# A two-layer transformer kernel: the second layer's attention and FFN worked through in pairs of batches instead of single batches

## The chip, the cores and the metric

The kernel runs on one core of a Trainium2 chip. Times are device microseconds (us) of that core for one execution of the whole program. The kernel before takes 736.29 us (median of three runs, 736.03 to 736.33). All data are f32.

A core has several engines that each work through a queue of their own in order: TensorE (PE; the profile lists its weight loads as PEld), VectorE (DVE), ScalarE (ACT), GpSimd (POOL), and SyncE (SP), on whose queue this kernel issues its DMAs. An instruction that waits holds up everything behind it in its own queue. TensorE writes its results into PSUM; a *bank* is the unit of PSUM that the program's tiles are made of.

## What is computed

Four batches of 256 tokens with 256 channels go through two layers, each with attention and an FFN, each behind a layer norm and added to `x`:

```python
x = x + _L0_attn_ref(_layernorm(x), ...)   # 16 heads of 128, window of 128
x = x + _L0_ffn_ref(_layernorm(x), ...)    # silu(gate) * up, two of four kept, down
x = x + _L1_attn_ref(_layernorm(x), ...)   # 16 heads of 128, causal
x = x + _L1_ffn_ref(_layernorm(x), ...)    # silu(W1 x) * (W3 x), Hadamard transform, W2
```

The change touches the second layer. Its attention is

```python
k = jnp.einsum('ihd,bpd->biph', W_K, x)
q = jnp.einsum('ihd,bpd->biph', W_Q, x)
v = jnp.einsum('ihd,bpd->biph', W_V, x)
scores = jnp.einsum('biph,biqh->biqp', k, q)
...
attn = jax.nn.softmax(masked / jnp.sqrt(jnp.float32(d_head)), axis=-1)
z = jnp.einsum('biqp,biph->biqh', attn, v)
...
out = jnp.einsum('df,bqf->bqd', W_O, z_flat)
```

and its FFN is

```python
up_gate = jnp.einsum('bsd,hd->bsh', x, W1)
up_lin = jnp.einsum('bsd,hd->bsh', x, W3)
hidden = fwht(jax.nn.silu(up_gate) * up_lin)
out = jnp.einsum('bsh,dh->bsd', hidden, W2)
```

## The kernel before

**Seven products.** Layer 2's projections are done by a scheme that multiplies two 2×2 block matrices with seven block products instead of eight (`seven_products`, L662–689). Its products are numbered 1 to 7; `left_of` (L636) makes the sums of blocks of the normed, transposed `x` on DVE, `right_of` (L647) those of the weights. Each product goes into one of three PSUM tiles `x`, `y`, `z`, some on top of what is there; ACT copies (`u`, L671–677) and DVE adds (L680–686) take the four result blocks out between the products.

**Attention.** There are 16 units: one batch and a group of four heads, the batch changing fastest. `project1` (L870) makes a unit's q and k by seven products of four matmuls with 128 columns each (L881; the columns are half of a batch's tokens), and its v by seven of one matmul with 256 columns (L887). `probabilities` (L203) multiplies q and k (`sc`, L217/L218), takes the row maxima on DVE (`mx`, L220; `nb`, L225), exponentiates on ACT (L230), takes reciprocals of the sums on DVE (`rs`, L235) and scales on POOL (`p`, L238). `planes` (L247) splits the words on POOL (`pl`, L244) and issues a DMA transpose on SP's queue (`plT`). `joined` (L257) puts the words together again on ACT and DVE (`pT`, L264), and `values` (L270) multiplies with v (`av`, L272/L275). ACT copies the result to `zT`.

`pipelined` (L300) runs the units in steps: step s does project(s), score(s−1) and attend(s−2), and then whatever the dictionary `behind` has for that step. In steps 1 to 17 TensorE's order is as the program writes it; the order on the other engines, and everything in the second FFN, is set by a scheduler. The sums of weight groups 2 and 3 (`load_group1`) are put into a list and taken from it a few at a time between the products of later projections (`pull`). Group 2 is loaded in step 4, group 3 in step 8; each has two buffers in turn.

**Output projection.** For units 0 to 8 it goes by seven products of two matmuls with 128 columns (`out_by_seven`, L787–808), interleaved with project(4) to project(12); POOL makes their left sums (`left_of_z`), DVE adds each product's result to `x` (L807). Units 9 to 15 are projected plainly, eight matmuls of 256 columns in one PSUM bank, out of order: 12 behind step 15, 9 and 10 ahead of attend(14), 11 and 13 ahead of attend(15), and 14 and 15 at the end:

```python
for t in range(NT):
    for j in range(4):
        nc.tensor.matmul(po[:, t, :], lhsT=zT[:, j, t * P : (t + 1) * P], rhs=w[:, j, :], ...)
for t in range(NT):
    nc.vector.tensor_tensor(xt, po[:, t, :], xt, ALU.add)
```

**The way into the second FFN.** `normed` (L150–200) takes a batch's moments on DVE (`st`, `mv`), computes `ve` and `rstd` on POOL (L156/L157), normalises on DVE (`xn`, L171), and transposes: either on TensorE, or by splitting words on POOL (`xpl`), a DMA transpose (`xplT`) and joining on ACT (`xnT`, L197). Batch 0's norm is issued in step 16 by DMA, batch 1's in the first FFN unit on TensorE.

**Second FFN.** Eight units, one batch and half of the 1024 hidden channels. `gated1` (L948) makes gate and up together, in seven products of four matmuls with 128 columns (L959), then silu on ACT and the product on DVE. `down` (L598) projects back, its two token halves in two PSUM banks, interleaved with the next unit's gate and up. W2 carries the Hadamard transform (`hadamard`), prepared during the attention.

Of the kernel before, what the change touches and what calls it, by code (L numbers as in the profile page):

```python
# [14 lines left out]

# [12 lines left out]
P = 128  # L28
# [3 lines left out]
HD = 128  # L32
# [16 lines left out]
def two_layers(ctx, tc, consts, tables, x, wq, wkv, wo, w_gate, w_up, w_down,  # L49
# [230 lines left out]
    def project_out1(po, zT, w, b):  # L280

        for t in range(NT):
            for j in range(4):
                nc.tensor.matmul(  # L284
                    po[:, t, :], lhsT=zT[:, j, t * P : (t + 1) * P], rhs=w[:, j, :],
                    start=(t == j == 0), stop=(j == 3), skip_group_check=True,
                )
        for t in range(NT):
            xt = xs[b * NT + t]
            nc.vector.tensor_tensor(xt, po[:, t, :], xt, ALU.add)  # L290

# [243 lines left out]
    def ffn0():  # L535
        hs, xn = {}, dict(enumerate(xn_f))
        for n in range(8):
            b, gc = divmod(n, 2)
            hs[n] = h = gated(xn[b], gate_sb, up_sb, 4 * gc, "h")
            a = page("a")  # L540
            nc.scalar.activation(a, h, AF.Abs)
            keep_two_of_four(a, h)
            if gc == 0 and b + 2 < B:
                xn[b + 2] = normed(b + 2, by_dma=True)
            if n >= 2:
                run(down(hs, n - 2, down_sb))
            if n == 4:
                xn1[0] = normed(0, by_dma=True)
            if n == 6:
                xn1[1] = normed(1, by_dma=True)  # L550
                left1[0] = left_of(xn1[0])
        return [down(hs, n, down_sb) for n in (6, 7)]
# [45 lines left out]
    def down(hs, n, w, last=False):  # L598


        b, gc = divmod(n, 2)
        if gc == 0:
            pos[b] = [bank([D], "po_f") for _ in range(NT)]
        for t in range(NT):
# [8 lines left out]
            if gc == 1:  # L613
                x = xs[b * NT + t]
                nc.vector.tensor_tensor(x, pos[b][t], x, ALU.add)
                if last:
                    at = (b * NT + t) * P
                    nc.sync.dma_start(out[at : at + P, :], x)
            yield

# [13 lines left out]
    def left_of(xnT):  # L634

        s = late.tile([P, 4, P], F32, tag="xs4", name="xs4", bufs=4)  # L636
        x11, x12, x21, x22 = (xnT[:, c, t * P : (t + 1) * P] for t in range(2) for c in range(2))
        for i, a, b, op in (
            (0, x21, x22, ALU.add), (1, s[:, 0], x11, ALU.subtract),
            (2, x11, x21, ALU.subtract), (3, x12, s[:, 1], ALU.subtract),  # L640
        ):
            nc.vector.tensor_tensor(s[:, i], a, b, op)
        return x11, x12, s[:, 3], x22, s[:, 0], s[:, 1], s[:, 2]
# [9 lines left out]
    def right_of(w11, w12, w21, w22, t, later=False):  # L653

        for i, a, b, op in (
            (0, w12, w11, ALU.subtract), (1, w22, t[0], ALU.subtract),
            (2, w22, w12, ALU.subtract), (3, w21, t[1], ALU.subtract),
        ):
            if later:
                queue.append((t[i], a, b, op))  # L660
            else:
                nc.vector.tensor_tensor(t[i], a, b, op)  # L662
        return w11, w21, w22, t[3], t[0], t[1], t[2]

    def seven_products(product, x, z, y, c11, c12, c21, c22, shape, z_alone=True):


        tag = "u" if len(shape) == 3 else "uv"
        u = [late.tile(shape, F32, tag=tag, name="u", bufs=3) for _ in range(3)]
# [30 lines left out]
    def load_group1(g, later=False):  # L700
# [7 lines left out]
        qk_t = late.tile([P, 4, 2, 2, HD], F32, tag="qkt", name="t_qk")  # L708
        v_t = late.tile([P, 4, 2 * HD], F32, tag="vt", name="t_v")
        gw[g] = (  # L710
            right_of(*(qk[:, :, c, :, m, :] for c in range(2) for m in range(2)),
                     [qk_t[:, i] for i in range(4)], later),
            right_of(*(v[:, c, m, :] for c in range(2) for m in range(2)),
                     [v_t[:, i] for i in range(4)], later),
        )

    def attention1(finish_ffn0):
        left = left1

        def project(n, _):  # L720
            g, b = divmod(n, 4)
            held = project1(
                left[b], gw[g], out_by_seven(n - 4) if 4 <= n < 13 else None,
                {3: turn3} if n == 2 else {},
            )
            if n < 2:
                with tc.issue_after(last_of["sum"].ins):
                    left[b + 1] = left_of(xn1[b + 1])
# [5 lines left out]
            if b == 0 and 1 <= g < 3:  # L734
                load_group1(g + 1, later=True)
            return held

        def score(n, held):
            qk, v = held
            ps = [  # L740
                probabilities(qk[:, 0], qk[:, 1], heads, mask1) for heads in ((1, 3), (0, 2))
            ]
            return [planes(p, page_of_planes) for p in ps], v

        zTs, kept = {}, {14: (9, 10), 15: (11, 13)}

        def attend(n, held):
            ps, v = held
            for m in kept.get(n, ()):
                out(m, True)(zTs)  # L750
            if n in (1, 3, 5, 7):
                zT = late.tile([P, 4, T], F32, tag="zT1", name="zT1", bufs=1)
# [3 lines left out]
            for kk in range(2):  # L756
                pT = joined(ps[kk], ((nc.scalar.copy, slice(0, 2), None),) if n < 1 else (
# [4 lines left out]
                for j in range(2):  # L762
                    hd = 2 * j + 1 - kk
                    values(v[:, 0, hd, :], v[:, 1, hd, :], pT[:, j], av[:, j, :])
                nc.scalar.copy(zT.rearrange("p (j m) t -> p m j t", m=2)[:, 1 - kk], av)
            if n < 9:
                z_left[n] = left_of_z(zT, z_sums[:, n % 2])
# [4 lines left out]
        def left_of_z(z, s):  # L772
            x11, x12, x21, x22 = (
                z[:, 2 * k : 2 * k + 2, t * P : (t + 1) * P] for t in range(2) for k in range(2)
            )
            for i, a, b, op in (
                (0, x21, x22, ALU.add), (1, s[:, 0], x11, ALU.subtract),
                (2, x11, x21, ALU.subtract), (3, x12, s[:, 1], ALU.subtract),
            ):
                nc.gpsimd.tensor_tensor(s[:, i], a, b, op)  # L780
            return x11, x12, s[:, 3], x22, s[:, 0], s[:, 1], s[:, 2]

        def right_of_out(g):
            w, t = w_out[g], w_sums[:, g % 2]
            w_right[g] = right_of(
                *(w[:, 2 * k : 2 * k + 2, m * P : (m + 1) * P] for k in range(2) for m in range(2)),
                [t[:, i] for i in range(4)], later=True,  # L787
            )

        def out_by_seven(n):  # L790


            g, b = divmod(n, 4)
            left, right = z_left[n], w_right[g]
            sums = bank([3, P], "po1")
            x, y, z = (sums[:, i, :] for i in range(3))
            for o, i, t, m in (
# [3 lines left out]
                for j in range(2):  # L801
                    nc.tensor.matmul(  # L802
                        o, lhsT=left[i - 1][:, j, :], rhs=right[i - 1][:, j, :],
                        start=(i == 1 and j == 0), stop=(j == 1), skip_group_check=True,
# [4 lines left out]

        def load_ffn1(_):  # L810
# [3 lines left out]

        def out(n, kept=False):
            g, b = divmod(n, 4)

            def emit(done):
                if not kept:
                    project_out1(bank([NT, D], "po1"), done[n], w_out[g], b)  # L820
                else:
                    with tc.issue_after(last_of[1].ins):
                        project_out1(st([P, NT, D], "po1"), done[n], w_out[g], b)
            return emit
# [10 lines left out]
        def left3(_):  # L835
            with tc.issue_after(last_of["mx"].ins):
                left[3] = left_of(xn1[3])

        behind = {step: [lambda _, g=g: right_of_out(g)] for g, step in enumerate((0, 3, 8))}
        behind[0].append(lambda _: run(finish_ffn0[0]))  # L840
        behind[1] = [lambda _: run(finish_ffn0[1]), norm3]
        behind[2] = [left3]
        behind[8].insert(0, lambda _: load_out(2))
        behind[12] = [load_ffn1, lambda _: load_out(3)]
# [5 lines left out]
        behind.setdefault(11, []).append(prepare)  # L850
        for i in range(12):
            behind.setdefault(11 + i // 4, []).append(
# [3 lines left out]
        def prepare_ffn1(half):  # L856
# [6 lines left out]
        behind.setdefault(15, []).append(out(12))  # L863
        behind[16] = behind.get(16, []) + [
            lambda _: xn_f.append(normed(0, by_dma=True)),
            prepare_ffn1(1),
        ]
        behind[17] = [out(14), out(15)]
        pipelined((project, score, attend), (0, 1, 2), behind, (0, 1, 2), (1, B * 4 + 2))
# [4 lines left out]
    def project1(x, w, between, others):  # L874
        wqk, wv = w
        qk = late.tile([P, 2, 4, T], F32, tag="qk", name="qk1")
        v = late.tile([P, NT, 4, HD], F32, tag="v", name="v1", bufs=3)

        def product_qk(o, i, first):
            for j in range(4):  # L880
                last_of[1] = nc.tensor.matmul(  # L881
                    o[:, j, :], lhsT=wqk[i - 1][:, j // 2, j % 2, :], rhs=x[i - 1],
# [3 lines left out]
        def product_v(o, i, first):  # L886
            last_of[1] = nc.tensor.matmul(  # L887
                o, lhsT=x[i - 1], rhs=wv[i - 1], start=first, stop=True, skip_group_check=True
            )

        c = qk.rearrange("p k (a m) (t c) -> p (k a) m t c", m=2, t=NT)
        products = [seven_products(
            product_qk, *(st([P, 4, P], f"qk_{n}") for n in "xzy"),
            *(c[:, :, m, t, :] for t in range(2) for m in range(2)), [P, 4, P],
        )]
        c = v.rearrange("p t (m j) h -> p t m (j h)", m=2)
# [3 lines left out]
            *(c[:, t, m, :] for t in range(2) for m in range(2)), [P, 256], z_alone=False,  # L900
# [42 lines left out]
    def factors_ffn1(half):  # L943

        t = late.tile([P, 2, 4, 2, P], F32, tag="qkt", name="t_gu")
        r = []
        for i, w in enumerate((w1_sb, w3_sb)):
            w = w[:, :, 4 * half : 4 * half + 4, :].rearrange("p c (a m) f -> p c a m f", m=2)  # L948
            r.append(right_of(*(w[:, c, :, m, :] for c in range(2) for m in range(2)),
                              [t[:, i, k] for k in range(4)], half == 0))  # L950
        return r

    def gated1(x, r, last, between):

        def product(o, i, first):
            for j in range(4):
                nc.tensor.matmul(  # L959
# [142 lines left out]
```

## Time and profile before

| | |
|---|---|
| median of three runs | 736.29 us |
| the profiled execution, its own time | 736.55 us |
| its span | 734.6 us |
| first layer (to about 355 us) | 355 us, PE busy 347.5 |
| 355 to 400 us, the attention's first steps | 45 us, PE busy 44.08 |
| 400 to 620 us, its later steps | 220 us, PE busy 220.00 |
| 620 to 652.4 us, its end | 32.4 us, PE busy 32.32 |
| 652.4 us to the end, second FFN | 82.2 us, PE busy 79.19 |

The span is what lies between the first and the last instruction that the profiler recorded; the time of the same execution is 1.95 us longer. Busy time of an engine in a stretch says how much room it has there: an engine that is busy all of a stretch sets its length, whatever the others do. The last 3.4 us of the span, in which TensorE is done, are the last addition and the transfer of the output.

In the views of the profile, a line of a timeline gives the start, the length, the engine, the line of the program, the operation, the tiles written and read, shape, and how many records are merged in it. What stands in brackets is the time the engine was idle before it, and what ended that. A matmul's own length includes the time that its last results need to arrive; the next one may start before, so that the pitch from start to start is what a stream of them costs. An f32 matmul shows as two records.

### The profile page before, as it was taken

How to read it: one execution, taken by the hardware profiler on the slowest of the kernel's cores; microseconds unless marked ns; L12 is line 12 of the kernel's file. 1: busy time of each engine (PE TensorE's matmuls, PEld its weight loads, DVE VectorE, ACT ScalarE, POOL GpSimd, SP SyncE). 2: the span in 40 equal slices, each digit the busy share in tenths (PEclk: the TensorE clock that was granted, in tenths of full speed). 3: DMA queues.
4: the chain of work that ended last, by engine and by line, in shares of the span. 5: the costliest groups of instructions: out<-in, count | busy, mean ns of one | idle time of the engine just before them, and what ended most of it. 6: DMA issues, size and time to landing. Idle time of an engine off the chain costs nothing.

```text
span 734.6 us, 11900 instructions
## 1 busy us (share of the span) xinstructions
PE 723.1 (98%) x4020; PEld 595.2 (81%) x4020; DVE 478.2 (65%) x1455; ACT 410.4 (56%) x985; POOL 368.0 (50%) x525
## 2 busy tenths in 40 slices
PE   8999999999999999999999999999999999999998
PEld 5556576656666778888988999999998998899997
DVE  6999877887887537987744565556553655454443
ACT  2487887667767952222257555555555676434332
POOL 1588878897799631011115655445446675520000
PEclk9999999999999999999999999999999999999999
DMA  8732344425445445000203632352233522501100
GB/s 324 298 65 49 60 89 85 93 52 94 83 82 101 73 99 202 16 14 15 67 7 62 150 52 54 45 158 44 44 64 56 155 44 45 97 6 22 27 11 30
DMA packets 138349, 57.53 MB, mean 78 GB/s; under 512 B 131504, under 2 KB 133680, under 8 KB 137520
## 3 DMA queue, kind: packets, MB, share of 16 engines
q1 hardware_dynamic: 138288, 56.77, 34.1%
q8 instruction: 32, 0.52, 0.3%
q14 instruction: 29, 0.24, 0.1%
HBM read 22.94 MB, written 1.05 MB: 33 GB/s over the span
## 4 chain that ended last, share of the span: by engine, by line
PE 82%; DVE 8%; issue 4%; ACT 3%; POOL 1%; DMA 1%; SPq 0%; ACTq 0%; DVEq 0%; POOLq 0%
PE pj L457 10%; PE pgu L561 8%; PE po L296 7%; PE qk_x L881 6%; PE po_f L606 6%; PE sc L218 6%; PE gu_x L959 4%; PE po L802 4%; PE av L272 4%; PE po L284 3%; PE av L405 3%; PE qk_y L881 3%; PE v_x L887 3%; PE sc L217 3%; PE v_zy L887 2%
## 5 line engine op out<-in xcount | busy, mean ns | idle before, releaser
L238 POOL TENSOR_SCALAR p<-p,rs 128x128 f32<-128x128 f32 (+1 forms) x256 | 113.6, 463 | 136.3 <-DVE rs L235 136.3
L264 ACT COPY pT<-plT 128x1536 uint16<-128x1536 uint16 (+1 forms) x62 | 90.0, 1508 | 15.7 <-DMA plT<-pl 15.7
L244 POOL TENSOR_SCALAR pl<-p 128x1536 uint16<-128x1536 uint16 x64 | 94.3, 1474 | 4.5 <-POOL p L238 0.5
L220 DVE CUSTOM_DVE_ANT_0 p<-sc,cst 128x128 f32<-128x128 f32 (+1 forms) x256 | 78.7, 352 | 10.0 <-PE sc L218 7.4
L230 ACT ACTIVATE p<-p,nb,r 128x128 f32<-128x128 f32 (+1 forms) x128 | 68.2, 534 | 20.2 <-DVE nb L227 20.2
L457 PE MATMUL pj<-wq,xnT 128*128 128x512 f32 x128 | 61.0, 595 | 1.7 <-DVE qT L519 1.1
L230 ACT ACTIVATE p<-p,nb 128x128 f32<-128x128 f32 (+1 forms) x128 | 56.3, 441 | 9.6 <-DVE nb L225 9.6
L457 PE MATMUL pj<-wkv,xnT 128*128 128x512 f32 x128 | 60.1, 592 | 0.0
L296 PE MATMUL po<-wo,zT 128*128 128x256 f32 x256 | 57.9, 379 | 0.0
L467 ACT ACTIVATE sq<-pj 128x512 f32<-128x512 f32 (+1 forms) x64 | 30.9, 489 | 42.6 <-DVE qc L462 42.3
L689 ACT COPY qk<-qk_x 128x512 f32<-128x512 f32 x16 | 9.4, 585 | 81.0 <-PE qk_x L881 81.0
L296 PEld LDWEIGHTS po<-wo,zT 128*128 128x128 f32 x256 | 48.3, 190 | 7.0 <-ACT kT L530 0.6
L156 POOL TENSOR_SCALAR ve<-mv 128x2 f32<-128x2 f32 (+1 forms) x17 | 4.3, 254 | 89.0 <-DVE mv L152 88.5
L457 PEld LDWEIGHTS pj<-wkv,xnT 128*128 128x128 f32 x128 | 24.3, 190 | 30.2 <-issue 28.5
L462 DVE TENSOR_TENSOR qs<-pj,sin_s 128x512 f32<-128x512 f32 (+1 forms) x64 | 35.3, 551 | 13.5 <-PE pj L457 12.9
L807 DVE TENSOR_TENSOR x<-po,x 128x128 f32<-128x128 f32 x63 | 18.0, 286 | 39.6 <-PE po L802 39.6
L457 PEld LDWEIGHTS pj<-wq,xnT 128*128 128x128 f32 x128 | 23.5, 190 | 24.7 <-issue 20.1
L244 POOL TENSOR_SCALAR qpl<-qc 128x1024 uint16<-128x1024 uint16 x20 | 28.8, 1452 | 18.9 <-PE av L409 8.2
L272 PE MATMUL av<-pT,v 128*128 128x256 f32 x128 | 38.3, 381 | 0.0
L218 PE MATMUL sc<-kT,qT 128*128 128x256 f32 x128 | 38.3, 381 | 0.0
L218 PE MATMUL sc<-qk 128*128 128x256 f32 x128 | 38.2, 380 | 0.0
L500 POOL TENSOR_TENSOR r<-ve,mhalf 128x12 f32<-128x12 f32 x16 | 36.6, 2290 | 0.8
(171 smaller groups left out, 1847.7 us busy)
## 6 DMA issues: line engine op xcount, KB each, us to landing
w<-in_w_dram SPq DMA_DIRECT2D x3, 1024.0 KB, 4.9
wq<-in_wq_dram SPq DMA_DIRECT2D x4, 512.0 KB, 7.5
wkv<-in_wkv_dram SPq DMA_DIRECT2D x4, 512.0 KB, 8.1
wo<-in_wo_dram SPq DMA_DIRECT2D x4, 512.0 KB, 10.3
w_qk<-in_w_q_dram SPq DMA_DIRECT2D x4, 512.0 KB, 4.6
w_qk<-in_w_k_dram SPq DMA_DIRECT2D x4, 512.0 KB, 5.2
w_v<-in_w_v_dram SPq DMA_DIRECT2D x4, 512.0 KB, 6.0
w_o<-in_w_o_dram SPq DMA_DIRECT2D x4, 512.0 KB, 6.6
```

Of the source, the lines that this page charges most:

```text
L218: nc.tensor.matmul(sc[:, P : 3 * P], lhsT=q[:, P:T], rhs=k, start=True, stop=True)
L220: last_of["mx"] = nc.vector.tensor_tensor_reduce(out=p[:, j, cols], in0=sc[:, cols], in1=mask[:, cols], scale=1.0, scalar=-3.0e38, op0=ALU ...
L230: last_of["exp"] = nc.scalar.activation(p[:, j, cols], p[:, j, cols], AF.Exp, bias=nb[:, j, i : i + 1], scale=SCALE1 if rq is None else rq ...
L238: nc.gpsimd.tensor_scalar(p[:, j, cols], p[:, j, cols], rs[:, j, i : i + 1], 1.0, ALU.mult, ALU.mult)
L244: last_of["planes"] = nc.gpsimd.tensor_scalar(o, i, 1.0, 1.0, ALU.mult, ALU.mult)
L264: copy(words.rearrange("p (n w) -> p w n", w=2), halves[:, :, js].rearrange("p w j n -> p w (j n)"),)
L272: nc.tensor.matmul(av, lhsT=v0, rhs=pT[:, 0:T], start=True, stop=False, skip_group_check=True)
L296: nc.tensor.matmul(po, lhsT=zTs[hd // 4][:, hd % 4, t * P : (t + 1) * P], rhs=w[:, hd, :], start=(hd == 0), stop=(hd == n - 1),)
L457: last_of[0] = nc.tensor.matmul(pj, lhsT=xnT[:, c, t * P : (t + 1) * P], rhs=w[:, g, c, :], start=(c == 0), stop=(c == NC - 1),)
L561: nc.tensor.matmul(o[:, j, :], lhsT=w[:, c, f0 + j, :], rhs=xnT[:, c, :], start=(c == 0), stop=(c == NC - 1),)
L606: nc.tensor.matmul(pos[b][t], lhsT=hs[n][:, j, t * P : (t + 1) * P], rhs=w[:, 4 * gc + j, :], start=(gc == 0 and j == 0), stop=(gc == 1 an ...
L881: last_of[1] = nc.tensor.matmul(o[:, j, :], lhsT=wqk[i - 1][:, j // 2, j % 2, :], rhs=x[i - 1], start=(first and j == 0), stop=True, skip_ ...
```

## The change

**Pairs.** A unit of the second attention is now two heads of a group in two batches, and there are still 16 units. A pair of consecutive units (k) is one group g and one pair of batches p: the order of (g, p) is (0,0), (1,0), (0,1), (1,1), (2,0), (2,1), (3,0), (3,1), so that the first two groups take turns. A q or k product is two matmuls with 256 columns in place of four with 128. The v of a group and a pair of batches is made by the two units together, one token half each, and its products stay one matmul of 256 columns. `left_of` makes its sums once for two batches. In the second FFN a unit is a pair of batches and half of the hidden channels, four in all; gate and up have seven products each, in turn, two matmuls of 256 columns per product.

**Output projection.** Eight projections, numbered 0 to 7 (pair k and batch j of the pair), go by seven in steps 5 to 12. Numbers 8 to 15 are plain: 8 behind step 12, 9 behind 13, 12 and 13 behind 15, 10 and 11 ahead of attend(15), 14 and 15 interleaved with the first FFN unit. Score(15) moves from step 16 into step 15, after attend(13). Block t=0 is added to `x` before block t=1 is multiplied, in the same PSUM bank; the second FFN's `down` does likewise, with one bank for both halves (the first FFN keeps the old one as `down0`).

**Blocks and loads.** Sums that nobody reads the original of any more overwrite it: `w12` in `right_of`, `x21` in `left_of`, so three blocks of sums in place of four. Groups 2 and 3 are loaded behind project(5) and project(7). W2 is loaded behind step 10 instead of ahead of the attention. All of the second FFN's norms transpose by DMA; those of batches 0 and 1 are issued together in step 16.

```diff
-    def project_out1(po, zT, w, b):
+    def project_out1(po, heads, w, b):
         for t in range(NT):
-            for j in range(4):
+            for j, z in enumerate(heads):
                 nc.tensor.matmul(
-                    po[:, t, :], lhsT=zT[:, j, t * P : (t + 1) * P], rhs=w[:, j, :],
+                    po[:, t, :], lhsT=z[:, t * P : (t + 1) * P], rhs=w[:, j, :],
                     start=(t == j == 0), stop=(j == 3), skip_group_check=True,
                 )
-        for t in range(NT):
+                if j == 1:
+                    yield
             xt = xs[b * NT + t]
             nc.vector.tensor_tensor(xt, po[:, t, :], xt, ALU.add)
+            yield
...
     def down(hs, n, w, last=False):
+        p, half = divmod(n, 2)
+        for k in range(2):
+            b = 2 * p + k
+            if half == 0:
+                pos[b] = bank([NT, D], "po_f")
+            for t in range(NT):
+                for j in range(4):
+                    nc.tensor.matmul(
+                        pos[b][:, t, :], lhsT=hs[n][k][:, j, t * P : (t + 1) * P],
+                        rhs=w[:, 4 * half + j, :], start=(half == t == j == 0),
+                        stop=(half == 1 and j == 3), skip_group_check=True,
+                    )
+                    if j == 1:
+                        yield
+                if half == 1:
+                    x = xs[b * NT + t]
+                    nc.vector.tensor_tensor(x, pos[b][:, t, :], x, ALU.add)
+                    if last:
+                        at = (b * NT + t) * P
+                        nc.sync.dma_start(out[at : at + P, :], x)
+                yield
...
-        for i, a, b, op in (
-            (0, w12, w11, ALU.subtract), (1, w22, t[0], ALU.subtract),
-            (2, w22, w12, ALU.subtract), (3, w21, t[1], ALU.subtract),
+        for piece in (
+            (t[0], w22, w12, ALU.subtract), (w12, w12, w11, ALU.subtract),
+            (t[1], w22, w12, ALU.subtract), (t[2], w21, t[1], ALU.subtract),
         ):
...
     def attention1(finish_ffn0):
+        def unit(n):
+            k, a = divmod(n, 2)
+            g, p = (k % 2, k // 2) if k < 4 else divmod(k, 2)
+            return g, p, a
+
         def project(n, _):
-            g, b = divmod(n, 4)
-            held = project1(
-                left[b], gw[g], out_by_seven(n - 4) if 4 <= n < 13 else None,
+            g, p, a = unit(n)
+            qk, vs[g, p, a] = project1(
+                left[p], gw[g], a, out_by_seven(*divmod(n - 5, 2)) if 5 <= n < 13 else None,
                 {3: turn3} if n == 2 else {},
             )
...
-            if b == 0 and 1 <= g < 3:
-                load_group1(g + 1, later=True)
-            return held
+            if n in (5, 7):
+                load_group1((n - 1) // 2, later=True)
+            return qk
...
+        def score_last(_):
+            scored[15] = score(15, qk_of[15])
...
-        zTs, kept = {}, {14: (9, 10), 15: (11, 13)}
+        zTs, kept, qk_of = {}, {15: (10, 11)}, {}
...
+        behind[10].extend((lambda _: load_out(2), load_w2))
+        behind[12].extend((load_ffn1, lambda _: load_out(3), out(8)))
+        behind[13].append(out(9))
...
-        behind.setdefault(15, []).append(out(12))
-        behind[16] = behind.get(16, []) + [
-            lambda _: xn_f.append(normed(0, by_dma=True)),
+        behind[15].extend((score_last, out(12), out(13)))
+        behind[16].extend((
+            lambda _: xn_f.extend(normed(b, by_dma=True) for b in range(2)),
             prepare_ffn1(1),
-        ]
-        behind[17] = [out(14), out(15)]
-        pipelined((project, score, attend), (0, 1, 2), behind, (0, 1, 2), (1, B * 4 + 2))
+        ))
+        pipelined((keep_qk, score, attend), (0, 1, 2), behind, (0, 1, 2), (1, B * 4 + 2))
+        return chain(*(product_out(n, bank([NT, D], "po1")) for n in (14, 15)))
...
         def product_qk(o, i, first):
-            for j in range(4):
+            for j in range(2):
                 last_of[1] = nc.tensor.matmul(
-                    o[:, j, :], lhsT=wqk[i - 1][:, j // 2, j % 2, :], rhs=x[i - 1],
+                    o[:, j, :], lhsT=wqk[i - 1][:, j, a, :], rhs=x[i - 1],
                     start=(first and j == 0), stop=True, skip_group_check=True,
                 )
...
         for n in range(4):
             p, half = divmod(n, 2)
             hs[n] = []
             if n:
                 before = down(hs, n - 1, w2h[0], last=True)
             g, u = (late.tile([P, 4, 2, T], F32, tag="qk", name=name) for name in ("gate", "up"))
             for at, _ in enumerate(gated1(left[p], r_ffn1[half], g, u)):
                 fill(before, {3: 1, 5: 1, 7: 1, 9: 1, 11: 1, 12: 1}.get(at, 0))
                 if at == 11:
                     gate(n, 0)
                     product(n, 0)
                 if n == 1 and at == 9:
                     left[1] = left_of(xn[2], xn[3])
             gate(n, 1)
             product(n, 1)
             run(before)
```

## Prediction

> **What bounds the kernel now.** I read the page's busy shares first, then busy time by stage, then TensorE's timeline, and last the queues of POOL and DVE where the second attention ends.
>
> ```profile
> PE 723.1 (98%) x4020; PEld 595.2 (81%) x4020; DVE 478.2 (65%) x1455; ACT 410.4 (56%) x985; POOL 368.0 (50%) x525
> ...
> PE 82%; DVE 8%; issue 4%; ACT 3%; POOL 1%; DMA 1%; SPq 0%; ACTq 0%; DVEq 0%; POOLq 0%
> ```
>
> ```profile
> 480.00:620.00 140.00, 140.00 (x994) 131.10 (x993) 77.00 (x303) 83.56 (x239) 77.76 (x108) 1.00 0.35 77
> 620.00:652.40 32.40, 32.32 (x162) 28.46 (x162) 16.65 (x61) 13.51 (x36) 16.51 (x28) 1.00 0.33 57
> ```
>
> TensorE (first pair of figures after the length) is busy all 140.00 us of the attention's later part and 32.32 of the 32.40 us that lead into the second FFN, at granted clock 1.00; DVE, ACT and POOL have about half their time free. So a shorter TensorE stream is worth what it saves, and whatever makes TensorE wait is added in full. The second half of the program holds no hidden reserve: its lost TensorE time, added up gap by gap from 355 us on, is about 3.8 us.
>
> ```profile
> 605.32 1.06 PE L881 MATMUL qk_x<-xnT,w_qk 128*128 128x128 f32 x8
> 606.21 0.60 PE L887 MATMUL v_x<-w_v,xnT 128*128 128x256 f32 x2
> ...
> 614.59 0.38 PE L217 MATMUL sc<-qk 128*128 128x128 f32 x2
> ...
> 619.93 3.62 PE L284 MATMUL po<-w_o,zT 128*128 128x256 f32 x16
> ...
> 626.35 7.07 PE L284 MATMUL po<-w_o,zT 128*128 128x256 f32 x32
> 633.26 0.59 PE L272 MATMUL av<-pT,v 128*128 128x256 f32 x2
> ...
> 652.31 0.94 PE L959 MATMUL gu_x<-xnT,w 128*128 128x128 f32 x7
> ```
>
> From starts to starts: eight records at 128 columns take 606.21 − 605.32 = 0.89 us, 0.1117 each over a whole unit; 32 records at 256 take 633.26 − 626.35 = 6.91, 0.216 each. An f32 matmul is two records. The plain projections (L284) run on without a pause, the two halves of one behind each other.
>
> **The stream.** Matmuls of 128 columns go from 1140 (140 of them one-record transposes) to 450 (136), of 256 from 776 to 1120; 512 stays at 164. Records: 2000 to 628 at 128, 1552 to 2240 at 256, and 4 transposes fewer. −1372 × 0.1117 = −153.2; +688 × 0.2158 = +148.5; −4 × 0.11 = −0.4: **−5.2 us**. It is TensorE time, so on the path. Within it: 112 q/k products at 0.030 give 3.4, 56 gate/up products 1.7, and the ninth projection that is no longer by seven products costs 0.3 (16 × 0.216 − 28 × 0.1117).
>
> [...]
>
> **Removed.** The eight gate/up units each lose 0.05 us and four short waits of the second FFN (about 0.4) go with the transposes on TensorE: **−0.8**, between 0 and −1.2.
>
> **Added: the halves of a plain projection share a PSUM bank with the add between them.** Before, both halves were multiplied and then both added (L280–290). Now DVE adds block t=0 to x before t=1's first matmul may write the same bank. That wait is new. Its price when DVE is free: the last matmul drains 0.17 beyond its pitch (0.38 against 0.216), DVE starts some 0.05 later, adds for 0.42 (L615's row; L290's two take 0.76), and the release takes about 0.07: **0.7 us**. For out(8) and out(9), alone behind steps 12 and 13: **+1.4**. Lower end 0, if other work filled TensorE, but its order there is as written and nothing stands between the halves; upper end 2 × 1.3, if each add meets one `mx` chain half (1.32) in DVE's queue.
>
> [...]
>
> **Where the price is not 0.7: the end of the attention.** Score(15) moves from step 16 into step 15, straight after attend(13), and out(12), out(13) follow. In the new instruction order DVE has, between out(12)'s and out(13)'s adds, the two `xn` of batch 0's norm. They wait for `rstd` on POOL, and in POOL's queue `rstd` stands behind all softmax work of units 14 and 15. Behind out(13)'s first add waits TensorE, and behind TensorE attend(14), out(10), out(11).
>
> ```profile
> 620.21 2.13 POOL L238 TENSOR_SCALAR p<-p,rs 128x128 f32<-128x128 f32 x4 [8.54 <-DVE rs L235]
> ...
> 623.87 1.63 POOL L238 TENSOR_SCALAR p<-p,rs 128x128 f32<-128x128 f32 x4
> 625.59 1.47 POOL L244 TENSOR_SCALAR pl<-p 128x1536 uint16<-128x1536 uint16 x1
> ...
> 638.20 0.71 POOL L157 TENSOR_TENSOR rstd<-ve,mhalf 128x2 f32<-128x2 f32 x1
> ```
>
> ```profile
> 616.46 0.28 DVE L220 CUSTOM_DVE_ANT_0 p<-sc,cst 128x128 f32<-128x128 f32 x1
> ...
> 638.94 0.74 DVE L171 TENSOR_SCALAR xn<-x,mv,rstd 128x256 f32<-128x256 f32 x2 [5.50 <-POOL rstd L157]
> 639.60 0.75 DVE L290 TENSOR_TENSOR x<-po,x 128x256 f32<-128x256 f32 x2
> ```
>
> Already before, DVE sat 5.50 us at `xn` with an output add behind it; TensorE didn't care, because no matmul waited for that add. Count from the start of score(14), 614.59 before. Softmax on POOL starts at +5.62 (620.21); its first unit ends at +12.47 (625.59 + 1.47). The second unit needs two more halves of 3.17 (1.64 + 1.47 and a gap): +18.8. `ve` and `rstd` 0.19 + 0.71: +19.7. Two `xn`, 0.74: +20.4; the add 0.42: +20.9. If DVE starts `mx` earlier than the 1.87 us of before, up to 0.5 comes off. TensorE resumes at about +20.6. It would have got there at 3 × 2.62 (score, attend, score) + 3.45 + 1.73 = +13.05: **7.6 late**. What is late next: out(10)'s add stands behind batch 1's `xn`, which wait on POOL's `ve`, `rstd`, `xpl` of that moment, 0.7; the first gate product goes on; out(11)'s add stands behind `left_of` (four DVE operations at about 0.4), which waits for batch 1's joined transpose: POOL ends `xpl` at +27.5, 3.0 for the DMA, 1.25 for ACT, 1.6 and 0.42 for DVE, +33.9 against an arrival at +31.8: 1.9 with its release. In all 10.2, less 0.4 lost in this stretch before: **+9.8**. Low end 4 × 0.7 = 2.8; if `rstd` came before out(12) it would be that. High end 13, if batch 1's transpose meets two landings at 4.2 and ACT's two `pT` copies at 1.91.
>
> **Other edits.** The last `down` pairs its halves in one bank too. Cover from other batches' rows hides part: **+0.7**, from 0.3 to 1.4. Steps 2 to 4 are shorter in TensorE (14.31 against 14.51) while the loop from one `mx` to the next takes 14.6 to 14.9 on DVE: **+0.4**, 0 to 1.5. The loads of groups 2 and 3 now start after project(5) and project(7), whose predecessors still read the buffer. Landing takes 4.6 to 6.0, and DVE gets to their first sums some 3.4 after the load is issued, so it stands there about 2 us with `nb` and `rs` behind it. Their chain has about 2.6 us of slack in a step with a by-seven projection (17.4 against 14.75), so **+0.3**; without that cover 2 × 2 = 4. The in-place sums and three blocks in place of four are DVE and POOL work beside a full TensorE, nothing; without that cover, 0.69 us per 512-column operation. w2's load, moved to step 10, has a step of 17 us ahead of its first reader: nothing; its landing of 4.9 is the price without it.
>
> **Sum.** 736.55 (span 734.6, and 1.95 around it) − 5.2 − 0.8 + 1.4 + 9.8 + 0.7 + 0.4 + 0.3 = 743.15; the median of the runs, 736.29, lies 0.26 lower: **742.9**.
>
> **Rivals.** (A) The bank waits cost only their own add, because POOL and DVE reach the norm in time. 736.55 − 6.0 + 6 × 0.7 + 1.4 = 736.2, range 734.8 to 740. For it: DVE is half idle at 620 to 652. Against it: POOL's queue, which needs four halves of 3.17 first. (B) Faster. One mechanism, at out(12) and out(13): the second half's matmul meets a finished add, because what is ahead of the add on DVE has drained before TensorE comes there. TensorE then loses nothing and the stream decides: 736.55 − 6.0 + 0.3 = 730.8, up to 734.8 with a few adds uncovered. It decides if `rstd` ends before +11 and not +19.7, so if softmax for two units took 4 us of POOL instead of 13. (C) DVE's standing at the loads of groups 2 and 3 isn't covered: +4, 747. For it: landings up to 6.0; against it: 2.6 us of slack. A fourth, that the pairs save no TensorE time, is the first term at 0: 748.
>
> **How the numbers follow.** Forecast 740 to 746: 0.65; A 0.13; B 0.11; C and above 0.11. 8 in 10: 736 to 747. A measurement here tells no change from change at about 0.2%, 1.5 us: faster is below 734.8 (B and the edge of A), 0.13; the same up to 737.8, 0.06; slower 0.81.
>
> **What would show it.** Right: q/k and gate products at 128x256 with four records in 0.86; a TensorE gap of about 7 us inside the `po` rows of out(13), released by DVE `x`, with DVE's `xn` released by POOL `rstd` just before; smaller gaps of 0.7 at out(8), out(9). Wrong: `po` rows at 0.216 throughout, or `rstd` ahead of the `p` and `pl` rows of unit 15. The forecast falls if the gap at out(13) is under 3 us or if losses in steps 2 to 8 pass 4 us.

## The result, and the profile after

The changed kernel takes 744.13 us (median of four runs, 743.4 to 744.75) against 736.31 us before (736.03 to 736.33): a ratio of 1.0107, with a 95% interval of 1.0089 to 1.0124. It is slower by 7.8 us, where 742.9 was forecast. The profiled execution took 744.64 us, its span 742.9, 8.3 more than before.

From the page of the changed kernel, the busy time of each engine, and the shares of the chain of work that ended last:

```profile
PE 723.2 (97%) x3332; PEld 574.3 (77%) x3332; DVE 476.7 (64%) x1425; ACT 414.5 (56%) x985; POOL 367.3 (49%) x523
...
PE 49%; issue 19%; POOL 19%; DVE 8%; ACT 3%; DMA 1%; SPq 0%; POOLq 0%; ACTq 0%; DVEq 0%
```

TensorE has 688 records fewer and the same busy time, 723.2 against 723.1: what the wider matmuls saved has come back, partly as records that ran at half clock (below). In the chain that ended last, POOL went from 1% to 19% and `issue` from 4% to 19%. Followed back, this chain goes over to POOL's queue at the end of the attention and stays there back to about 363 us, most of that in a stretch in which TensorE is busy for 218.5 of 220 us; so the share says where the chain passes and not what POOL costs. That is read from the rows below.

Busy time by stage, for the same two stretches as before (the first pair of figures after the length is TensorE; the third figure from the right is the granted clock):

```profile
400.00:620.00 220.00, 218.50 (x1206) 195.18 (x1205) 119.98 (x447) 125.96 (x355) 120.53 (x172) 1.00 0.37 81
620.00:652.40 32.40, 25.76 (x114) 20.32 (x113) 15.53 (x58) 19.54 (x45) 16.96 (x28) 0.93 0.36 66
```

The first lost 1.5 us, the second 6.6, and its clock is 0.93. The end of the attention on TensorE, from the start of score(14) at 617.10 (in brackets the idle time and who ended it):

```profile
617.10 0.39 PE L218 MATMUL sc<-qk 128*128 128x128 f32 x2
...
626.25 1.13 PE L285 MATMUL po<-w_o,zT 128*128 128x256 f32 x4 [0.61 <-DVE mx L221]
628.61 1.13 PE L285 MATMUL po<-w_o,zT 128*128 128x256 f32 x4 [1.23 <-ACT zT L813]
630.26 5.41 PE L285 MATMUL po<-w_o,zT 128*128 128x256 f32 x16 [0.52 <-DVE x L292]
637.33 1.99 PE L285 MATMUL po<-w_o,zT 128*128 128x256 f32 x8 [1.66 <-DVE x L292]
...
644.18 3.72 PE L285 MATMUL po<-w_o,zT 128*128 128x256 f32 x16 [0.52 <-DVE x L292]
647.74 1.03 PE L1011 MATMUL gu_x<-xnT,w 128*128 128x256 f32 x4
650.62 3.21 PE L285 MATMUL po<-w_o,zT 128*128 128x256 f32 x8 [1.85 <-DVE x L292]
```

In this stretch an output projection stops four times after its first half until DVE has added it (`x`, L292). At 637.33 it is out(13). Its add on DVE, and what that stood behind on POOL:

```profile
634.55 0.18 DVE L153 BATCH_NORM_AGGREGATE mv<-st 128x2 f32<-128x6 f32 x1
636.20 0.74 DVE L172 TENSOR_SCALAR xn<-x,mv,rstd 128x256 f32<-128x256 f32 x2 [1.47 <-POOL rstd L158]
636.85 0.42 DVE L292 TENSOR_TENSOR x<-po,x 128x256 f32<-128x256 f32 x1
```

```profile
633.63 1.47 POOL L245 TENSOR_SCALAR pl<-p 128x1536 uint16<-128x1536 uint16 x1
635.19 0.19 POOL L157 TENSOR_SCALAR ve<-mv 128x2 f32<-128x2 f32 x1
635.46 0.70 POOL L158 TENSOR_TENSOR rstd<-ve,mhalf 128x2 f32<-128x2 f32 x1
```

Read upwards: the last `pl` of unit 15 ends at 635.1, then come `ve` and `rstd`, then DVE's `xn`, then the add, then TensorE at 637.33. Score(14) began at 617.10, so that is 20.2 us behind it. Batch 0's `mv`, which `ve` also needs, was there at 634.73, 0.4 ahead of POOL.

TensorE's span divides into records at their usual pitch and time lost against it (gaps, and records at a longer pitch). At 0.1117, 0.2158 and 0.429 us a record (128, 256 and 512 columns), its records take 714.6 us before and 709.5 after. The lost time went from 16.8 to 30.1. By place:

| | forecast | measured |
|---|---|---|
| stream of matmuls | −5.2 | −5.2 |
| short waits of the second FFN | −0.8 | −1.0 |
| out(8), out(9) | +1.4 | +1.6 |
| end of the attention | +9.8 | +11.5 |
| last `down` | +0.7 | +0.8 |
| steps 2 to 4 | +0.4 | +0.8 |
| loads of groups 2 and 3 | +0.3 | 0.0 |
| first layer | 0 | −0.3 |
| sum (span) | +6.6 | +8.2 |

(The spans are 734.64 and 742.85 before rounding.)

### The profile page after: what moved, and what is told of

Its sections match the earlier page's. It is cut to its first block, busy times and chain, and to the rows that moved or that the text cites. A ratio compares the mean times of both kernels' runs of the same rounds, so it can differ in the third digit from the quotient of the medians.

```text
span 742.9 us, 10479 instructions
## 1 busy us (share of the span) xinstructions
PE 723.2 (97%) x3332; PEld 574.3 (77%) x3332; DVE 476.7 (64%) x1425; ACT 414.5 (56%) x985; POOL 367.3 (49%) x523
## 4 chain that ended last, share of the span: by engine, by line
PE 49%; issue 19%; POOL 19%; DVE 8%; ACT 3%; DMA 1%; SPq 0%; POOLq 0%; ACTq 0%; DVEq 0%
PE pj L460 10%; PE pgu L564 7%; POOL p L239 7%; PE po L299 7%; POOL pl L245 5%; PE po_f L611 4%; PE gu_x L1011 4%; PE av L408 3%; PE po_f L634 3%; PE sc L219 2%; POOL z_sums L675 2%; PE gu_y L1011 2%; PE po L285 2%; PE av L412 2%; DVE p L221 1%
## 5 line engine op out<-in xcount | busy, mean ns | idle before, releaser
L265 ACT COPY pT<-plT 128x1536 uint16<-128x1536 uint16 (+1 forms) x62 | 93.5, 1564 | 7.2 <-DMA plT<-pl 7.2
L285 PE MATMUL po<-w_o,zT 128*128 128x256 f32 x128 | 34.3, 413 | 7.4 <-DVE x L292 5.6
L245 POOL TENSOR_SCALAR qpl<-qc 128x1024 uint16<-128x1024 uint16 x20 | 28.8, 1450 | 19.1 <-PE av L412 8.3
L850 DVE TENSOR_TENSOR x<-po,x 128x128 f32<-128x128 f32 x56 | 16.0, 285 | 33.1 <-PE po L845 33.1
```

The lines of the kernel that those rows point to most:

```text
L245: last_of["planes"] = nc.gpsimd.tensor_scalar(o, i, 1.0, 1.0, ALU.mult, ALU.mult)
L265: copy(words.rearrange("p (n w) -> p w n", w=2), halves[:, :, js].rearrange("p w j n -> p w (j n)"),)
L285: nc.tensor.matmul(po[:, t, :], lhsT=z[:, t * P : (t + 1) * P], rhs=w[:, j, :], start=(t == j == 0), stop=(j == 3), skip_group_check=True,)
```

## Experiments

Ten kernels were run, on three chips, each with the kernel before beside it; ratios are to that. The kernel before took 736.43 us beside the adds behind both halves, the dependence put into the kernel before, out(13) ahead of out(12), and the spare matmuls in out(11) alone; 735.12 beside the last two of this section; 736.53 beside the other four.

**The adds behind both halves.** The new dependence is taken out of the output projection (the second FFN's `down` keeps it): TensorE writes both halves of the bank, and then DVE adds both, as in the kernel before.

```diff
-            xt = xs[b * NT + t]
-            nc.vector.tensor_tensor(xt, po[:, t, :], xt, ALU.add)
-            yield
+            if t < NT - 1:
+                yield
+        for t in range(NT):
+            xt = xs[b * NT + t]
+            nc.vector.tensor_tensor(xt, po[:, t, :], xt, ALU.add)
+        yield
```

> Changed kernel, but a plain output projection multiplies both token halves and then adds both, as the kernel before did. Theory (TensorE's second half waits for an add that DVE holds back behind the norm): the waits at out(8), out(9) (0.78 each), out(12), out(13) (1.92), out(10), out(11) (2.12) and the two stretches of TensorE at half clock (1.7 and 1.4 us) go, 10 us in all: 734, with about 3 us still lost around score(15) and out(12). Rival (score(15) put ahead of out(12) is what costs, since out(12) then waits for ACT): 740 or more. Rival (only the add itself costs, 0.7 each): 740.

734.58 us, ratio to before 0.9977 (0.9968 to 0.9986). This one edit takes 9.6 us off the changed kernel's 744.13. TensorE's timeline in the same place:

```profile
624.29 1.13 PE L285 MATMUL po<-w_o,zT 128*128 128x256 f32 x4 [0.62 <-DVE mx L221]
626.65 6.31 PE L285 MATMUL po<-w_o,zT 128*128 128x256 f32 x28 [1.23 <-ACT zT L816]
...
635.41 7.07 PE L285 MATMUL po<-w_o,zT 128*128 128x256 f32 x32
```

Out(10) and out(11) run as one block of 32 records in 7.07 us, and out(13) joins out(12) without a pause. DVE still stands 3.06 us for POOL's `rstd` at 634.24 with out(13)'s adds behind it, and nobody on TensorE asks for them. What remains is 2.9 us around score(15) and out(12). The first theory stands, and both rivals (740) are out; score(15)'s new place alone accounts for no more than these 2.9.

**The same dependence, put into the kernel before.** Nothing else of the change.

```diff
-        for t in range(NT):
             xt = xs[b * NT + t]
             nc.vector.tensor_tensor(xt, po[:, t, :], xt, ALU.add)
```

(The two lines that stay move into the loop over t that multiplies.)

> The kernel before with one part of the change: in its plain output projections, block t=0 is added to x ahead of t=1's matmuls in the same bank. Theory: six of the seven projections pay 0.7 to 0.8, and out(10)'s add stands in DVE's queue behind batch 0's norm, which is ready at about 638.9 us: TensorE gets there at 633 and stands until 640.6, 7.6 us, perhaps with a stretch at half clock behind it (0 to 1.7): 748, between 745 and 751. Rival (only the add itself costs): 736.3 + 7 x 0.75 = 741.5. Rival (new waits come from the pairs, not from this): 737.

744.86 us, ratio 1.0116 (1.0101 to 1.0131): 8.4 us more from one edit; both rivals (741.5 and 737) are out. The size was just under the range that was expected (745 to 751), and the place was another. In this kernel's order on POOL, `rstd` (632.03) comes ahead of unit 15's softmax (from 633.82), and `xn` was no obstacle. In the kernel before it came behind it, at 638.20: the scheduler orders POOL anew, so what this run shows is the dependence together with the order that the scheduler then chose. TensorE:

```profile
631.63 3.72 PE L284 MATMUL po<-w_o,zT 128*128 128x256 f32 x16 [2.96 <-DVE x L289]
...
644.98 3.72 PE L284 MATMUL po<-w_o,zT 128*128 128x256 f32 x16 [2.77 <-DVE x L289]
```

and DVE ahead of the first of them:

```profile
630.67 0.61 DVE L264 COPY pT<-plT 128x768 uint16<-128x768 uint16 x1 [2.31 <-DMA plT<-pl]
631.17 0.41 DVE L289 TENSOR_TENSOR x<-po,x 128x256 f32<-128x256 f32 x1
```

Here the add stood behind a copy of the softmax that waited 2.31 us for its DMA transpose; 644.98 is the same with the other half. Out(12) and out(10), whose adds stood behind nothing, paid 0.78 each. So the price is 0.78 plus whatever DVE's queue happens to hold ahead of the add, and that needn't be the norm.

**Out(13) ahead of out(12).**

```diff
-        behind[15].extend((score_last, out(12), out(13)))
+        behind[15].extend((score_last, out(13), out(12)))
```

> Changed kernel with out(13) ahead of out(12), nothing else. Batch 0's norm then waits for the second of them, so that no add of either stands behind it. Theory: out(12) and out(13) pay 0.7 each and no more, out(10) about 0.8, out(11) 1.2, and TensorE stays at full clock: 738.5, between 737 and 741. Rival (the order of DVE's queue doesn't matter, the bank wait itself does): 744, as the changed kernel.

741.65 us, ratio 1.0074 (1.0059 to 1.0089): 2.5 less than the changed kernel, where 5.6 were expected and 0 by the rival; it lies above the expected range of 737 to 741. Out(12) and out(13) paid 0.78 each, about as expected. But out(10)'s add now stood behind batch 1's norm, for 2.36 us, and out(11) lost 1.6:

```profile
641.66 0.73 DVE L172 TENSOR_SCALAR xn<-x,mv,rstd 128x256 f32<-128x256 f32 x2 [2.00 <-POOL rstd L158]
642.31 0.42 DVE L292 TENSOR_TENSOR x<-po,x 128x256 f32<-128x256 f32 x1
```

Both norms came late: batch 0's `mv` was ready at 637.7, 2.7 us after POOL had finished the softmax, because out(12) now came second; batch 1's `ve` and `rstd` stood behind batch 0's norm on POOL. The order of DVE's queue matters, and a swap only chooses who stands in it.

**Score(15) back in step 16.**

```diff
-        behind[15].extend((score_last, out(12), out(13)))
+        behind[15].extend((out(12), out(13)))
```

> Changed kernel with score(15) back in step 16, behind out(13); the halves of the projections still share a bank. Theory (DVE's queue): out(13) still waits for the norm of batch 0, but rstd now stands behind one unit's softmax on POOL and not two, so about 1.5 us there; 0.8 at out(12), out(10), out(11); and attend(15) stands 2 to 6 us for its own softmax, which starts later. 740, 737 to 742. Rival (the moved score(15) is itself what cost the 11.9 us at the end of the attention): 734 or less.

742.02 us, ratio 1.0079 (1.0064 to 1.0094), just at the upper end of what the first expectation allowed (737 to 742); the rival's 734 is out. Out(13) waited 1.9 for the norm, out(11) 2.6, with a stretch at half clock behind it (records at 256 columns 0.425 apart) that cost 1.6; attend(15) did not wait, unlike expected. Moving score(15) is not what costs most: taken back, it gives 2.1 us.

**Spare matmuls in the waits.** If TensorE only stands until DVE is done, work put into the wait is free. First in out(11) alone (five matmuls on zeroes, result unused, behind t=0):

```diff
+                if filler and (t, j) == (0, 3):
+                    spare = st_pool.tile([P, 2, T], F32, tag="st", name="spare")
+                    for i in range(filler):
+                        nc.tensor.matmul(spare[:, i % 2, :], lhsT=zeroes[:, 0:P], rhs=zeroes,
+                                         start=True, stop=True, skip_group_check=True)
```

> Changed kernel with five spare matmuls of 256 columns (2.2 us, on a tile of zeroes, result unused) between the two halves of out(11), where TensorE stood 2.0 us and then ran at half clock for 3.4 us. Theory (the wait ends when DVE is done, so the spare matmuls fit in; and the clock fell because TensorE had stood): clock 1.00 after it, 1.2 to 1.7 us less: 742.6. Rival (the clock has nothing to do with the standing): no gain or up to 0.3 more, 744 to 744.5. Rival (the wait isn't set by DVE): 2.2 more, 746.

746.39 us, ratio 1.0129 (1.0112 to 1.0146). That is the number of the third line of the expectation (the wait isn't set by DVE), but not its cause, for TensorE had done the spare matmuls and stood until DVE's add was there:

```profile
650.17 2.32 PE L294 MATMUL spare<-zeroes 128*128 128x256 f32 x10
653.12 1.99 PE L285 MATMUL po<-w_o,zT 128*128 128x256 f32 x8 [0.63 <-DVE x L297]
```

The clock stayed at 1.00 behind out(11). But in this execution TensorE got to out(13) at full clock, stood there 3.5 us, and fell to half clock behind that:

```profile
636.00:638.00 2.00, 0.00 (x0) 0.00 (x0) 0.91 (x3) 1.38 (x1) 0.89 (x2) 0.99 0.42 81
638.00:640.00 2.00, 1.79 (x4) 1.51 (x5) 0.77 (x3) 0.52 (x1) 0.00 (x0) 0.50 0.63 116
```

In the changed kernel the same fall (0.69 and 0.50 in the slices from 630 to 634 us) lay ahead of out(13)'s wait, where it cost nothing. Out(13) resumed 20.2 us behind score(14)'s start, as there; but its second half, from which batch 1's norm starts, now ran at half clock, and out(11) resumed 35.2 behind it rather than 33.5. The gain behind out(11) was lost there, and 0.87 more because the first gate product no longer ran in out(11)'s wait. So the three longest stands were filled together: 3 matmuls in out(12), 7 in out(13), 5 in out(11).

> Changed kernel with spare matmuls of 256 columns on zeroes, result unused, in its three longest stands of TensorE: 3 in out(12) ahead of its second pair of heads, 7 between the halves of out(13), 5 between the halves of out(11). If the half clock comes from TensorE standing (in the kernel with out(11) alone filled it fell behind the unfilled 3.5 us stand at out(13) instead), the granted clock is 1.00 throughout. Theory (ends of the waits at out(13) and out(11) are set by POOL, DVE and DMA, 20.2 and 33.5 us behind the start of score(14)): both resume at these times as before, and only the 1.4 us of half clock behind out(11) are gained: 742.7, 742 to 744. Rival (the half clock had nothing to do with standing): 0.5 in the rows again somewhere, 744 to 746.

744.28 us, ratio 1.0115 (1.0101 to 1.0129). The forecast gain to 742.7 did not come; 15 spare matmuls, 6.5 us of TensorE time, cost nothing against 744.13. The profiled execution was the longest of four (746.68; it lost 2.9 us more in the first layer, where its clock fell, to 0.62 in the slice from 24 to 28 us), so its times lie 2.8 later than the changed kernel's:

```profile
629.07 1.13 PE L285 MATMUL po<-w_o,zT 128*128 128x256 f32 x4 [0.61 <-DVE mx L221]
...
640.14 1.99 PE L285 MATMUL po<-w_o,zT 128*128 128x256 f32 x8 [0.32 <-DVE x L297]
...
653.49 1.99 PE L285 MATMUL po<-w_o,zT 128*128 128x256 f32 x8 [0.61 <-DVE x L297]
```

From out(12)'s start, out(13) resumes after 11.07 (11.08 in the changed kernel) and out(11) after 24.42 (24.37). TensorE ran at full clock all through this stretch (1.00 from 626 to 658 us), did 6.5 us more, and both waits ended at the same moment: their ends are not TensorE's. The other three runs had a clock of 0.999 to 1.000, the changed kernel's four 0.995 to 0.997. The 1.7 us of half clock behind out(11) are gone, but 0.87 went back, since the first gate product now ran behind out(11) rather than in its wait; the medians don't show the remaining 0.8, and why stays open.

**Towards a kernel that beats both.** The adds behind both halves, and in the second FFN's projection back (`down`) the two batches of a pair take turns, so that the next matmuls go to the other batch's bank:

```diff
-        for k in range(2):
-            b = 2 * p + k
...
-            for t in range(NT):
+        for t in range(NT):
+            for k in range(2):
+                b = 2 * p + k
                 for j in range(4):
```

> Adds behind both halves in the output projection, and in the second FFN's last projection the two batches take turns half by half, so that an add falls beside the other batch's matmuls. Theory: the one-bank wait at the end (0.78) goes too: 733.8, 0.8 below the kernel with the adds behind alone. Rival (the end is set by the last add and transfer): 734.6, no gain.

733.99 us, ratio 0.9968 (0.9957 to 0.998). The last `down` runs without a pause (44 records from 720.27 on in 9.66 us; 10.44 in the changed kernel). Against the kernel before, that is 2.5 us less, where the adds behind alone gave 1.9; the runs of the two overlap.

Then out(10) ahead of score(15), with `kept` reduced to out(11):

```diff
-        behind[15].extend((score_last, out(12), out(13)))
+        behind[15].extend((out(10), score_last, out(12), out(13)))
```

> As the last, and out(10) moves ahead of score(15), so that ACT has copied unit 13's result when out(12) needs it, and score(15)'s banks are free. Theory: the 2.9 us still lost around score(15) and out(12) go, but batch 1's norm then has 3.45 us less cover behind it and 0 to 2 come back ahead of the first gate product: 731.5, 731 to 733.5. Rival (nothing gained because the softmax of unit 15 gets late and attend(15) waits for it): 734 to 737.

735.64 us, ratio 0.9989 (0.998 to 0.9998): the expectation fell, the rival was right. The 2.9 us went, and came back behind it:

```profile
641.09 0.67 PE L273 MATMUL av<-pT,v 128*128 128x256 f32 x2 [0.64 <-ACT pT L265]
644.18 0.70 PE L273 MATMUL av<-pT,v 128*128 128x256 f32 x2 [1.54 <-ACT pT L265]
649.57 1.99 PE L1015 MATMUL gu_y<-xs,w 128*128 128x256 f32 x8 [1.81 <-DVE xs L679]
```

Attend(15) now waits for its softmax, and the second FFN for batch 1's norm. A projection taken from there took its cover along. Out(9), which covers nothing where it was, in its place:

```diff
-        behind[13].append(out(9))
...
+        behind[15].extend((out(9), score_last, out(12), out(13)))
```

> Adds behind both halves, turns in the last projection, and out(9) moves from behind step 13 to ahead of score(15). Theory: out(9)'s 3.45 us give DVE and ACT the time that score(15) and out(12) waited for (3.0 us lost in the two kernels with the adds behind), and nothing that follows gets less cover, unlike with out(10): 731, 730.3 to 732.3, a little lost in step 13 whose DVE loop (14.75) then is longer than TensorE's 14.31. Rival (the softmax of unit 15 gets late as it did with out(10), and attend(15) waits): 734 to 736.

733.14 us (before beside it: 735.12), ratio 0.9962 (0.9949 to 0.9976): no gain over the kernel with the turns (0.9968) that could be told from none. On a chip where the kernel before takes 1.4 us less, the forecast 731 would have had to be lower still; the expectation fell, though not into the rival's 734 to 736. In the profiled execution, the longest of five (731.56 to 734.59), nothing is left of the waits around score(15), but 1.2 us came up in the step that lost out(9), 0.7 at attend(14), 0.9 at out(11) and 0.8 at the second FFN, together more than was gained. In the last kernel three spare matmuls fill out(12)'s wait instead:

> Adds behind both halves and turns in the last projection, with three spare matmuls (1.3 us) where out(12) waits 1.5 us for unit 13's copied result. In the kernel without them two runs of six had a mean clock of 0.997 or 0.998 and took 734.9 and 735.0, the four at 1.000 took 733.3 to 734.2. Theory (standing lets the clock fall, in some runs): all runs at 0.999 or more and within 733.2 to 734.3, median 733.7. Rival (the fall has nothing to do with it): some runs at 0.997 and 735 again.

732.4 us (before: 735.12), ratio 0.9965 (0.9952 to 0.9977). All five runs had a mean clock of 1.000, from 732.18 to 733.75. With the 1.4 us that this chip is faster, the median is within 0.1 of the one forecast. That agrees with the theory; five runs against two falls in six are a small sample, and the ratio is not to be told from that of the kernel without the spare matmuls.

## Why the prediction was right, step by step

**The stream** was worth −5.2, as forecast. The records are those counted (2240 at 256 columns, 764 at 128, 328 at 512), and the pitch at 256 columns holds in the changed kernel (eight records of gate and up from 657.62 to 659.35, 0.216 each).

**The shared bank** cost 0.78 where nothing stood ahead of the add, against a forecast 0.7. With halves at different columns of one bank, TensorE's second half waited for DVE's add of the first and cost 0.78; with both adds behind both halves it cost nothing (32 records in 7.07 us without a pause). No run let the second half go ahead of an add that stands before it in the program, so whether it could is not shown.

**The end of the attention** was the main term, and its mechanism is shown: the changed kernel without the dependence loses 9.6 us less, the kernel before with it alone loses 8.4 more, and filling all three stands moves the end of neither wait. `rstd` was forecast to end 19.7 us behind the start of score(14) and ended at 19.1; TensorE was to go on in out(13) at 20.6 and did at 20.2, in the changed kernel and in both kernels with spare matmuls, whether it had come there at full or at half clock. The moment in out(11) was forecast at 33.9, and was 33.5. (The terms given for it add up to 33.8, and an arrival at 31.8 leaves 2.0 rather than 1.9.)

Two things in it were mis-sized. The forecast put all 7.6 us ahead of +20.6 at out(13), and said that it would fall if the gap there were under 3 us. The gap was 1.92. The delay up to that moment was 7.3 all the same, but the rest of it lay in five places ahead: 0.5 and 0.9 at score(15) and at out(12)'s bank, 1.5 at ACT's copy of unit 13, which stands behind unit 15's first exponentials, 0.8 at out(12)'s own halves, and 1.7 at half clock. Where a wait ends at a fixed moment, what is lost ahead of it shortens it; a test of one gap was the wrong test for it, and the moment was the right one. With the other stands filled, out(13) stood 3.6. Here the total owes something to luck: the prediction put the waits at score(15), at out(12)'s bank and at ACT's copy (2.9 us) and the half clock at nothing, and they cost nothing only because out(13)'s wait was long enough to take them in. Out(12)'s adds came late with them, and with those batch 0's `mv`, 0.4 us before POOL was free; with more lost, the moment itself would have moved. With the adds behind both halves these 2.9 us are lost in full.

And the step "out(11) [...] an arrival at +31.8: 1.9 with its release" left out that TensorE might not run at full clock behind a stand. The second fall, behind out(11) (0.50 at 652 to 654 us), cost 1.7, which is the difference between +9.8 and +11.5.

**The other edits.** Steps 2 to 4 cost 0.8, not 0.4: the same two waits as before (0.57 and 1.08 after, 0.42 and 1.03 before) and a third, 0.73 at 401. The loads of groups 2 and 3 cost nothing: no wait of more than 0.1 us stands on TensorE from 402 us to score(14) but those of out(8) and out(9). The waits taken out of the second FFN gave 1.0.

**The rivals.** A (the bank wait costs only its own add, 736.2) and B (the add is there in time, 730.8) asked for a queue on DVE that has drained; DVE's `xn` with 1.47 us of waiting for POOL answers it. With the dependence out of the output projection the time is 734.6, which is B's upper edge; its 730.8 would need the 2.9 us around score(15) and out(12) and the 0.78 of the last `down` gone as well. C (4 us at the loads, 747) found no wait there, and the fourth, that the pairs save nothing, is answered by the counts.

## What to carry to other kernels

Before an operation is put between two halves of a bank, look at what stands ahead of it in its engine's queue, not at its length: an add of 0.42 us cost 0.78 in one place and 3.2 in another. An engine at half load held up one that had been at full load, as soon as the full one had to wait for something at the end of its queue: DVE, busy for 15.53 of the 32.40 us from 620 us on, kept TensorE standing for 1.66 us at out(13). And cover is a thing that is used up: a piece of work moved to fill one wait opens another if something relied on it where it was.

## What the runs showed of the hardware

TensorE's clock fell to half after it had stood in several short pieces, with one core at work. In the 4 us ahead of 630 it was busy for 2.26 us, and its longest idle piece was 1.23 us. Granted clock (third figure from the right) in slices of 2 us of the changed kernel:

```profile
628.00:630.00 2.00, 1.13 (x4) 0.68 (x4) 0.22 (x1) 2.00 (x9) 2.00 (x5) 1.00 0.49 109
630.00:632.00 2.00, 1.74 (x5) 1.48 (x6) 0.85 (x4) 2.00 (x3) 1.91 (x3) 0.69 1.06 196
632.00:634.00 2.00, 2.00 (x6) 1.53 (x6) 0.38 (x1) 1.53 (x2) 1.91 (x5) 0.50 0.45 86
```

The pitch at 256 columns goes from 0.216 to 0.427, for about 3.4 us (1.24 at half clock in the second slice, 2.00 in the third, and a little of the next), and for as long again from about 651.2. Each of the two stretches costs 1.7 us. That standing brings it is supported by the runs with spare matmuls, in which the falls at the end of the attention went away (all three stands filled: 1.00 from 626 to 658 us) or moved to a stand that was not filled (out(11) alone filled: 0.50 at 638 to 640 us, behind out(13)'s 3.5 us). But it doesn't come with every stand: the kernel before with the bank shared stood 3.2 and 3.0 us at clock 1.00 in its profile, the kernel with out(10) ahead of score(15) stood 1.8 and 2.1 us and had a clock of 1.000 in eleven runs of eleven, and with the adds behind, eight runs of ten had a clock of 1.000 (733.69 to 734.74) and two 0.997 (735.87 and 735.91). The runs at the lower clock are some 1.4 us longer. How much standing brings the fall, no run here shows; that is left open.
